# Two buffers for the rotated parts of q and k, and a block's rest behind the next block's tail, in a fused transformer layer

## The chip, the cores and the metric

The kernel runs on one core of one Trainium2 chip. The metric is the device time of one execution in microseconds (us). Three runs of the kernel before took 3130.38, 3134.19 and 3142.39 us; the median is 3134.19 us.

## What is computed

The input is 16 batches of 512 tokens with 512 channels, all in 32-bit floats. Each batch passes through an attention layer and a feed-forward layer, each with a layer norm before it and one behind it (a "sandwich"):

```
x = x + layernorm(attention(layernorm(x)))
x = x + layernorm(ffn(layernorm(x)))

attention: q, k, v = x @ W.T + b            # 32 heads of 16 channels
           q, k = rope(rope(q)), rope(rope(k))   # two rotations by position
           softmax(q k^T / 4, causal) v, then @ Wo.T + bo
ffn:       silu(x gate^T * gate_s) * (x up^T * up_s), 1408 wide
           then @ down^T * down_s           # weights are -1, 0 or 1
```

The two rotations are folded into one table of cosines and sines, so that a rotated value is y * cos + swap(y) * sin, where swap exchanges the halves of a block of 128 channels.

## The kernel before, in words

**Engines and order.** The program is written for one core with five engines: TensorE (PE) multiplies, ScalarE (ACT) and VectorE (DVE) work on PSUM and SBUF, GpSimd (POOL) on SBUF, SyncE (SP) issues nearly all DMAs. Every instruction goes through `InOrder` (line 43), so each engine executes in the order of the program. That order is made by hand. The attention of batch b is cut into 8 groups of 4 heads, and each group into 5 steps (`one_step`, line 841). A step issues the score products of one group (`scores`, line 569: `st` for the weights, `s` for the row maxima) and then the next piece of a list of dense work (`run_list`, line 741), which shares the list out over the steps by cost: a matmul of q, k, v or o costs 1, one of gate, up or down 0.27, a transpose 0.15. The list that runs beside batch b holds the o product and the whole feed-forward of batch b-1 and the v, q and k products of batch b+1 (`dense`, line 504; `gate_ups`, line 755; `downs`, line 772). Inside `dense` the order is: 4 blocks of v, 4 of q, 4 of o, then 4 of k, each k block behind the transposes of one block of 128 tokens for the feed-forward.

**Deferred work.** `merge(L, f, after)` puts a function into the list that `laid` (line 483) places once `after` units of cost have gone by behind the point where it was merged. That is how the follow-up work of a block lands some matmuls later in every engine's order.

**A block of q or k** (`qk_block`, line 331) is 4 matmuls into one PSUM buffer of the pool `ps_d`, which has 3 buffers and also serves v, o, gate, up, down, the transposes (`px`) and the turned maxima (`pm`). Three functions follow:

- `tail`, with the last matmul: ACT writes both swapped halves with the bias into `ys`; DVE computes `ya` = (p + bias) * cos, which frees the PSUM buffer; POOL computes `ys` *= sin and `ya` += `ys`.
- `rest`, merged at 3: ACT copies `ya` into `yh`, rounded to the form that fast matmuls take; POOL computes the remainder `yl` = `ya` - `yh`.
- `store`, merged at 5.5: SP issues four DMAs, two for `yh` and two for `yl`, to DRAM (`qd` or `kd`), from where `load_group` (line 556) fetches them for the scores of the next batch.

`ya` and `ys` have one buffer each, `yh` and `yl` two each. The sums of the down product use a tag "y" of their own with two buffers (`down`, line 434); their stores go to the output.

**The row maxima.** DVE reduces the scores `s` into `nm` (line 648), PE turns them (`pm`), DVE splits them into `nmhl`, and SP puts them into `mx` (line 669) for the weights of the following group.

**The front** (line 861) runs before the first step: it normalizes and transposes batches 0 and 1, computes q and k of batch 0 block by block, and checks between the blocks that all feed-forward weights are unchanged by rounding (`check_weights`, line 200: an ACT copy and a DVE comparison for each piece). The comparisons end in a flag that selects between two versions of the rest of the program; with these weights it is the one with rounded operands. Batch 0's own list (`first_list`, line 937) holds the q and k of batch 1. At the end the last batch's dense work runs alone (`last_list`, line 813).

In `dense` and in `first_list` the two deferred parts of a block are placed by the same two lines:

```
self.merge(L, rest, 3)
self.merge(L, store, 5.5)
```

Of the kernel before, what the change touches and what calls it, by code (L numbers as in the profile page):

```python
# [18 lines left out]
P = 128  # L19
T = 512  # L20
# [37 lines left out]
class Block:  # L58
# [199 lines left out]
    def turn(self, tiles, key, tb, to, big):  # L258

        st = {}  # L260

        def go(c):
            if c == 0:
                st["p"] = self.psum("px")
            self.pe.transpose(st["p"][:, ts(c, P)], tiles[key, tb][:, ts(c, P)], self.ident)
            if c == NC - 1:
                del tiles[key, tb]
                p = st["p"].rearrange("p (c t) -> p c t", c=NC)
                if big == "xntf" and self.exact:
                    if tb == 0:  # L270
                        to[key] = [self.tile([P, NC, T], big + i, bufs=1, dtype=FR) for i in ("", "l")]
                    hi, lo = (t[:, :, ts(tb, P)] for t in to[key])
                    self.act.copy(hi, p)
                    self.dve.tensor_tensor(lo, p, hi, ALU.subtract)
                    return
                if tb == 0:
                    to[key] = self.tile([P, self.NF if big == "ht" else NC, T], big, bufs=1)[:, 0:NC, :]
                self.act.copy(to[key][:, :, ts(tb, P)], p)

        return [(TR, lambda c=c: go(c)) for c in range(NC)]  # L280
# [50 lines left out]
    def qk_block(self, b, name, c):  # L331

        bias = self.col["b" + name]
        st = {}

        def tail(p):
            ya = st["a"] = self.tile([P, T], "ya", bufs=1)
            ys = st["s"] = self.tile([P, T], "ys", bufs=1)
            for h in range(2):
                i, o = slice(64 * h, 64 * h + 64), slice(64 - 64 * h, 128 - 64 * h)  # L340
                self.act.activation(ys[o, :], p[i, :], AF.Identity, bias=bias[i, c : c + 1])
            self.dve.scalar_tensor_tensor(ya, p, bias[:, c : c + 1], self.cos, ALU.add, ALU.mult)
            self.pool.tensor_tensor(ys, ys, self.sin, ALU.mult)
            self.pool.tensor_tensor(ya, ya, ys, ALU.add)

        def rest():
            ya = st["a"]
            hi, lo = st["y"] = [self.tile([P, T], n, bufs=2, dtype=FR) for n in ("yh", "yl")]
            self.act.copy(hi, ya)
            self.pool.tensor_tensor(lo, ya, hi, ALU.subtract)  # L350

        def store():
            i = (b % 2) * NC + c
            for part, y in enumerate(st["y"]):
                if name == "q":
                    d = self.qd[i][:, part, :].rearrange("(h r) t -> h r t", r=DH)
                else:
                    d = self.kd[i][part].rearrange("(h r) t -> h r t", r=DH)
                for h in range(2):
                    self.sp.dma_start(out=d[:, 8 * h : 8 * h + 8, :], in_=y[64 * h : 64 * h + 64, :].bitcast(FP))  # L360

        return self.product(
            "p" + name, NC, lambda i: self.wts[b, name, c // 2][:, i, ts(c % 2, P)], lambda i: self.xnts["a", b][:, i, :], tail
        ), rest, store
# [139 lines left out]
    def dense(self, b, between=()):  # L504


        L = []
        nxt, old = b + 1 < self.B, b >= 1
        o, bn = b - 1, b + 1
        do = lambda f, *args: L.append((0, lambda: f(*args)))  # L510

        def qk(name, c):
            items, rest, store = self.qk_block(bn, name, c)
            L.extend(items)
            self.merge(L, rest, 3)
            self.merge(L, store, 5.5)

        if nxt:
            for tb in range(NB):
                L += self.v_block(bn, tb)  # L520
            for c in range(NC):
                if c < 2:
                    do(self.load_w, o, "o", c)
                qk("q", c)
                if c % 2:
                    do(self.load_w, bn, "k", c // 2)
        else:
            for half in range(2):
                do(self.load_w, o, "o", half)
        later = []  # L530
        if old:
            do(self.load_xr, o, 0)
            do(self.load_xr, o, 1)
            for tb in range(NB):
                items, *rests = self.o_block(o, tb)
                L += items
                for r, k in zip(rests, (3.5, 6.5, 9.5)):
                    if r is rests[2] and tb >= 2 and nxt:
                        later.append(r)
                    else:  # L540
                        self.merge(L, r, k, ("f", tb))
        L += between
        for c in range(NC):
            if old:
                if c < 2:
                    do(self.load_wf, o, c)
                L.append(("need", ("f", c)))
                L += self.turn(self.xns, ("f", o), c, self.xnts, "xntf")
                if c < len(later):
                    self.merge(L, later[c], 5, ("f", c + 2))  # L550
            if nxt:
                qk("k", c)
        return L
# [307 lines left out]
    def front(self):  # L861

        nc = self.nc
        self.load_checks()
        checks = self.check_weights()

        def check(n):
            for _ in range(min(n, len(checks) - 1)):
                checks.pop(0)()

        def norm(b, tb):
            xt = self.xts.pop((b, tb))
            mr = self.stats(xt)

            def rest():
                xn = self.xns[("a", b), tb] = self.tile([P, C], "sg" if b and tb >= 2 else "xn", bufs=2)
                if b == 0:
                    self.dve.tensor_scalar(xn, xt, mr[0], mr[1], ALU.mult, ALU.add)
                else:
                    self.scaled(xn, xt, mr)  # L880

            return rest

        def turn(b, tb):
            for _, f in self.turn(self.xns, ("a", b), tb, self.xnts, ("xnta", "xntf")[b]):
                f()

        rest = None
        for tb in range(NB):
            now = norm(0, tb)  # L890
            if tb:
                rest()
                turn(0, tb - 1)
            rest = now
        rest()
        turn(0, NB - 1)
        for k in range(2):
            r = [norm(1, 2 * k), norm(1, 2 * k + 1)]
            check(1)
            for f in r:  # L900
                f()
        rests = []
        for name in "qk":
            for c in range(NC):
                items, rest, store = self.qk_block(0, name, c)
                for _, f in items[:2]:
                    f()
                for f in rests:
                    f()
                for _, f in items[2:]:  # L910
                    f()
                rests = [rest, store]
                if name == "q" and 1 <= c < 3:
                    for k in range(2):
                        turn(1, 2 * (c - 1) + k)
                check(2)
            if name == "q":
                for half in range(2):
                    self.load_w(0, "v", half)
            else:  # L920
                self.sp.dma_start(out=self.xn1, in_=self.xnts["a", 1])
        for f in rests:
            f()
        check(len(checks))
        nc.vector.tensor_scalar_mul(self.gh, self.col["gs"], 0.5)
        nc.vector.tensor_tensor(self.gu, self.gh, self.col["us"], ALU.mult)
        for tb in range(NB):
            for _, f in self.v_block(0, tb):
                f()
            if tb == 2:  # L930
                checks.pop(0)()
        self.wts[1, "v", 0], self.wts[1, "v", 1] = self.wts[0, "v", 0], self.wts[0, "v", 1]
        for tb in range(2):
            for _, f in self.v_block(1, tb):
                f()

    def first_list(self):

        L = []
# [11 lines left out]
        def qk(name, c):  # L951
            items, rest, store = self.qk_block(1, name, c)
            L.extend(items)
            self.merge(L, rest, 3)
            self.merge(L, store, 5.5)

        for c in range(NC):
            if c < 2:
# [4 lines left out]
        for c in range(NC):  # L963
            st = {}
# [127 lines left out]
```

## Time and profile before

| | us |
|---|---|
| median of three runs | 3134.19 |
| the profiled execution | 3133.78 |
| its span in the trace | 3132.0 |
| TensorE busy / idle in the span | 3028.9 / 103.1 |
| VectorE, ScalarE, GpSimd busy | 1901.4, 1540.6, 1559.8 |
| one batch in the middle (from v block to v block) | 186.7 to 188.4 |
| the front, up to the last weight check | 74.6 |

The profile is one execution recorded by the hardware. A row of the wait table says which engine, about to write which buffer, stood idle until which engine had written which buffer, with the total in us, the number of times and the longest. In a row of a stretch (from:to), each engine's busy time is followed by its number of instructions in brackets; then come the granted clock of TensorE (1.00 is full), the mean busy share of the DMA engines and the GB/s. In the chain, each line is a start, a duration and what was done. PEld is the loading of weights into TensorE, which overlaps its matmuls. Nearly all instructions carry line 53, since one helper issues them all, so that buffers are told apart by their names: `pq` and `pk` are the PSUM buffers of q and k blocks, `px` of transposes, `ht` and `xntfl` in the front hold weights to be checked.

### The profile page before, as it was taken

Reading aid. Unit: us, or ns where it says so; the run is one execution under the profiler, and the core shown is the slowest. Engines: PE = TensorE matmul, PEld = TensorE weight load, DVE = VectorE, ACT = ScalarE, POOL = GpSimd, SP = SyncE. Lnnn points to the kernel's source line nnn. Section 1 sums busy time; section 2 is a strip of 40 time slices with the busy share of each in tenths; the row PEclk is TensorE's granted clock in tenths of the full one; section 3 lists DMA queues with packets and bytes.
Section 4 is the critical chain, followed back from the end, with each engine's and each line's share of the span. In section 5 each row is a group of like instructions: output and inputs, shape, how many; then the busy total and the mean of one; then the engine's idle time right before and its main releaser. Section 6 shows DMA issues by size and latency. Waiting matters only on the chain.

```text
span 3132.0 us, 58833 instructions
## 1 busy us (share of the span) xinstructions
PE 3028.9 (97%) x20746; PEld 1726.6 (55%) x20746; DVE 1901.4 (61%) x6042; ACT 1540.6 (49%) x2243; POOL 1559.8 (50%) x2313
## 2 busy tenths in 40 slices
PE   6989999999999999999999999999999999999998
PEld 3334655646556464655646556464655646555556
DVE  6565656656566665656666565665656666566733
ACT  5354555554544545545554554545455454554432
POOL 6244456453654635456463654635456463653442
PEclk9889999999999999999999999999999999999999
DMA  7454535445353544535445353543535445343432
GB/s 262 173 195 134 197 102 170 149 144 177 129 184 99 172 157 130 199 103 172 144 144 179 130 189 102 164 154 130 200 102 171 144 144 183 124 158 113 133 102 72
DMA packets 228464, 471.90 MB, mean 151 GB/s; under 512 B 40976, under 2 KB 46096, under 8 KB 227728
## 3 DMA queue, kind: packets, MB, share of 16 engines
q1 hardware_dynamic: 227728, 466.99, 45.0%
q8 instruction: 167, 2.74, 0.4%
q10 hardware_dynamic: 432, 1.05, 0.1%
q14 instruction: 137, 1.12, 0.1%
HBM read 345.79 MB, written 125.30 MB: 150 GB/s over the span
## 4 chain that ended last, share of the span: by engine, by line
PE 76%; POOL 9%; DVE 8%; ACT 3%; DMA 2%; issue 2%; SPq 0%; POOLq 0%; DVEq 0%; ACTq 0%
PE st L53 13%; PE pg L53 11%; PE pu L53 11%; PE pd L53 9%; PE av L53 8%; PE pq L53 7%; PE pv L53 7%; PE po L53 4%; PE s L53 3%; PE pk L53 3%; DVE ln_st L53 2%; POOL ln_mv L53 2%; POOL x L53 2%; ACT pt L53 1%; DVE s L53 1%
## 5 line engine op out<-in xcount | busy, mean ns | idle before, releaser
L53 DVE CUSTOM_DVE_ANT_0 s<-s,mask 128x512 f32<-128x512 f32 (+1 forms) x1782 | 872.1, 519 | 622.5 <-PE s L53 564.2
L53 ACT ACTIVATE pt<-st 128x1024 f32<-128x1024 f32 (+1 forms) x640 | 601.4, 940 | 789.3 <-PE st L53 532.5
L53 POOL TENSOR_SCALAR_AFFINE_SELECT pt<-pt 128x256 f32<-128x256 f32 x1024 | 402.8, 409 | 1047.1 <-ACT pt L53 1041.4
L53 PE MATMUL s<-kh,q 32*128 32x512 f32 (+1 forms) x1782 | 344.5, 386 | 12.0 <-DVE nm L53 10.0
L53 PE MATMUL av<-pt,v 128*32 128x512 f32 (+3 forms) x4096 | 332.8, 443 | 0.0
L53 POOL TENSOR_TENSOR hl<-ht,hh 128x512 fp32r<-128x512 f32 (+1 forms) x192 | 232.2, 1210 | 191.1 <-ACT hh L53 171.0
L53 PEld LDWEIGHTS st<-mx,one 2*128 2x128 f32 x1280 | 119.3, 183 | 371.7 <-issue 201.3
L53 PE MATMUL st<-mx,one 2*128 2x512 f32 (+1 forms) x1280 | 307.2, 476 | 16.5 <-ACT pt L53 7.6
L53 PE MATMUL s<-kl,q 32*128 32x512 f32 (+1 forms) x1782 | 302.1, 327 | 1.0 <-DMA kl<-kd 1.0
L53 PE MATMUL st<-q,kl 32*128 32x512 f32 (+3 forms) x1792 | 297.1, 326 | 0.0
L53 PE MATMUL pd<-wd,hl 128*128 128x512 f32 x704 | 289.1, 411 | 7.0 <-POOL hl L53 6.8
L53 PE MATMUL pg<-xntf,wf 128*128 128x512 f32 x704 | 286.1, 406 | 2.2 <-ACT xntf L53 2.2
L53 PE MATMUL st<-q,kh 32*128 32x512 f32 (+3 forms) x1792 | 287.7, 330 | 0.0
L53 PE MATMUL pd<-wd,hh 128*128 128x512 f32 x704 | 285.0, 405 | 2.2 <-ACT hh L53 2.2
L53 DVE DVE_READ_ACCUMULATOR2_ANT nm<- 128x1 f32 x2048 | 285.2, 139 | 1.4
L53 PE MATMUL pg<-xntfl,wf 128*128 128x512 f32 x704 | 284.6, 404 | 0.5 <-DVE xntfl L53 0.5
L53 PE MATMUL pu<-xntfl,wf 128*128 128x512 f32 x704 | 279.8, 397 | 0.0
L53 PE MATMUL pu<-xntf,wf 128*128 128x512 f32 x704 | 279.7, 397 | 0.0
L53 PE MATMUL pk<-xnta,w 128*128 128x512 f32 x480 | 246.4, 643 | 12.0 <-DVE ya L53 12.0
L53 PE MATMUL pq<-xnta,w 128*128 128x512 f32 x480 | 238.6, 629 | 6.7 <-ACT xntf L53 6.0
L53 PE MATMUL po<-w,oc 128*128 128x512 f32 x512 | 240.8, 607 | 4.0 <-DMA w<-in_wo 4.0
L53 PE MATMUL pv<-w,xnta 128*128 128x512 f32 x464 | 220.9, 612 | 3.3 <-DVE ya L53 2.7
(126 smaller groups left out, 5520.6 us busy)
## 6 DMA issues: line engine op xcount, KB each, us to landing
wf<-wgs SPq DMA_DIRECT2D x176, 512.0 KB
q<-qd SPq DMA_DIRECT2D x128, 256.0 KB
kh<-kd SPq DMA_DIRECT2D x128, 256.0 KB
kl<-kd SPq DMA_DIRECT2D x128, 256.0 KB
od<-ot SPq DMA_DIRECT2D x128, 256.0 KB
w<-in_wo SPq DMA_DIRECT2D x34, 512.0 KB
xr<-in_x SPq DMA_DIRECT2D x66, 256.0 KB
w<-in_wq SPq DMA_DIRECT2D x32, 512.0 KB
```

What stands on the lines that cost most here:

```text
L53: return self.tc.keep_in_program_order(f(*args, **kwargs))
```

## The change

The buffer `ya` takes the tag "y" of the down sums, with its two buffers, in place of a buffer of its own; `ys` gets two buffers. The memory used stays the same. In both lists a block's `rest` is merged at 4.2 instead of 3, which is behind the tail of the next block (after its last matmul if transposes lie in between, otherwise after the first matmul of the block after it), and its `store` at 6.5 instead of 5.5. In the front, the rest and store of a block come behind all four matmuls and the tail of the next block, and the transposes of batch 1 come ahead of the q blocks 1 and 2 instead of behind them.

```diff
         def tail(p):
-            ya = st["a"] = self.tile([P, T], "ya", bufs=1)
-            ys = st["s"] = self.tile([P, T], "ys", bufs=1)
+
+            ya = st["a"] = self.tile([P, T], "y", bufs=2)
+            ys = st["s"] = self.tile([P, T], "ys", bufs=2)
...
             L.extend(items)
-            self.merge(L, rest, 3)
-            self.merge(L, store, 5.5)
+
+            self.merge(L, rest, 4.2)
+            self.merge(L, store, 6.5)
...
         for name in "qk":
             for c in range(NC):
+                if name == "q" and 1 <= c < 3:
+                    for k in range(2):
+                        turn(1, 2 * (c - 1) + k)
                 items, rest, store = self.qk_block(0, name, c)
-                for _, f in items[:2]:
+                for _, f in items:
                     f()
                 for f in rests:
                     f()
-                for _, f in items[2:]:
-                    f()
                 rests = [rest, store]
-                if name == "q" and 1 <= c < 3:
-                    for k in range(2):
-                        turn(1, 2 * (c - 1) + k)
                 check(2)
```

The pair of `merge` lines changes in the same way in `first_list`.

More of the change, by code (lines that the diff above doesn't have):

```diff
@@ L953, in qk @@
             L.extend(items)
-            self.merge(L, rest, 3)
-            self.merge(L, store, 5.5)
+            self.merge(L, rest, 4.2)
+            self.merge(L, store, 6.5)
         for c in range(NC):
```

## The prediction

> **What bounds the kernel now.** I read the page first, then TensorE's (PE's) waits, then the span cut into batches, then the chain and five-microsecond windows around the one place where PE stands still, and last the front.
>
> ```profile
> span 3132.0 us, 58833 instructions
> ...
> PE 3028.9 (97%) x20746; PEld 1726.6 (55%) x20746; DVE 1901.4 (61%) x6042; ACT 1540.6 (49%) x2243; POOL 1559.8 (50%) x2313
> ```
>
> PE is the bound, and 103 us of its span are idle. A change that adds no PE work can gain only that idle time and time at a low clock. The waits of PE:
>
> ```profile
> engine line waited for: us in total, times, longest us
> PE s L53 <- DVE nm L53: 13.8, 28, 1.2
> PE pk L53 <- DVE ya L53: 13.0, 13, 1.0
> ```
>
> The second row is the change's own subject: 13 waits of 1.0 us, one in each of batches 1 to 13. Two batches side by side:
>
> ```profile
> core 0: us, PE busy (x) PEld busy (x) DVE busy (x) ACT busy (x) POOL busy (x), PEclk, DMA share, GB/s
> 437.93:624.67 186.74, 184.78 (x1297) 106.44 (x1297) 116.25 (x375) 95.28 (x139) 96.86 (x144) 1.00 0.46 152
> 624.67:813.09 188.42, 186.53 (x1298) 106.92 (x1297) 116.31 (x375) 95.18 (x139) 96.81 (x144) 0.99 0.46 150
> ```
>
> Both idle for 1.9 us. The second is 1.7 us longer because PE is *busy* 1.75 us longer for the same matmuls: the clock. Where that is:
>
> ```profile
> 699.00:704.00 5.00, 4.48 (x29) 2.11 (x27) 3.18 (x11) 3.58 (x5) 4.91 (x6) 1.00 0.24 82
> 704.00:709.00 5.00, 4.00 (x7) 1.63 (x6) 3.54 (x12) 2.22 (x4) 4.56 (x6) 0.66 0.14 41
> ```
>
> PE idles 0.52 us, then 1.00 us, and then runs at a granted clock of 0.66 over 5 us (0.52 in the 2.5 us from 705.0). POOL is full (4.91 of 5.00). The chain through it:
>
> ```profile
> 700.75 1.28 POOL ya L53
> 702.03 0.72 POOL pt L53 x2
> 702.75 0.01 issue
> 702.77 1.28 POOL yl L53
> 704.05 0.14 issue
> 704.19 0.76 DVE ya L53
> 704.95 0.04 issue
> 705.00 4.54 PE pk L53 x6
> ```
>
> This is the k phase (k0 to k3 of the next batch). k2's product is ready at 701.5. ACT, next in line for it, sits in k1's copy `yh` for `ya` (idle 1.34 us), so k2's `ys` run only from 702.71 to 704.10. DVE's `ya` of k2 then starts at 704.19, also held by k1's `yl` until 704.05, since there is one `ya`. Only that frees the PSUM buffer that k3 needs. The 0.52 us before it has the same root: DVE stood 2.84 us (to 699.48) for k0's `yl` with the reductions of `s` queued behind.
>
> **The change part by part.**
>
> *Two buffers and the rest behind the next tail, batches 1 to 13.* I walk the k phase again with the durations of these rows. k1's `ys` end at 697.87 as now; its `ya` no longer waits for k0's `yl`, so DVE is done at 698.65 instead of 700.2, and the 0.52 us go. POOL's order is now `ys`1, `ya`1, then `yl`0: 698.2 + 3 x 1.27 = 702.05. `ya`2 waits for that `yl`0 (two buffers back), but also for k2's `ys`, which ACT can start at 701.6 and end at 703.0; cover 0.9 us. `ya`2 ends at 703.75. PE reaches k3 at 704.0 - 0.5 = 703.5, so some 0.25 us of wait stay. Per batch: 1.00 + 0.55 - 0.25 = 1.3; times 13 = **17 us**. From both sides: 0, if `yl`0 comes over 1 us later than walked, and 20.
>
> *The clock.* In 2.5 us windows, 8 of these 13 batches show a stretch down to about half clock (near 330, 706, 894, 1269, 1644, 2019, 2207, 2582 us), each right after this stall and nowhere else in the batch. One costs 1.75 us (the two rows above): 14 us. Here the Trainium skill speaks against the gain: "TensorE: Matmul & The Clock Gate", section on HAM oscillation, gives as the rule that only PE gaps above some 3.4 us cool the clock, so a gap of 1 us should not, and taking it away should not help: then the sum ends at 3117. The trace has the low clock behind gaps of 0.5 and 1.0 us, 8 times in 13. I take the trace: **14 us**; bounds 0 and 14.
>
> *Batch 14* has two 0.6 us waits `s <- DVE nm` in its k phase and one such stretch (2774): 0 to 2.9, I take **1.5 us**, as their cause is not shown as clearly.
>
> *ACT's new order.* `yh` (0.62 us) now follows the next tail's two `ys` (1.38) directly, 2.0 us in one piece before the next `pt`, which frees the only `st` buffer. The nearest row is `PE st <- ACT pt`, 7.6 us in 18 waits. Against it: ACT no longer idles for `ya` (153.6 us in 95 waits), and that idling stood in front of the same `pt`. Bounds: -3 and +8 (0.6 x 13); I take **2 us lost**.
>
> *SP.* The four store DMAs move a unit later (some 1.25 us), but `yl` comes 2.6 us later (702.05 for 699.45). SP, which now stands 2.1 us for k0's `yl`, will stand about 4, to 702.05, plus 1.2 for the two issues. Behind it lie the `mx` puts, issued at 705.16 when their data are ready, so they do not move; first use is at 715.29, and the landing on the chain at 237.44 took 4.04 us, so 5 us of cover are left. The next group's loads (712.23) and `wf` (709.11) lie later still. **0**; without the cover each us would be a us of PE per batch.
>
> *The shared tag "y".* q0's `ya` takes the buffer of a down sum whose store went out two steps into the list, while 16 units of v lie in between (20 us). **0**. The split pieces keep six units between a store and the reuse of its buffer, where they had five: **0**.
>
> *Batch 0's own list (80 to 250 us).* No PE wait there comes from `ya`, ACT never waits for POOL, and the end of the list runs everything left in its last step in both versions, so the 3.8 us wait for `mx` at 237 stays. **0**; but about 22 us are lost there to half clock, whose phases can shift: -5 to +5.
>
> *The front (16 to 75 us).* Read as a chain, a k block takes 5.07 us (POOL 57.05 to 62.12), of which ACT's `yh` and two hand-overs lie between POOL's steps. With the rest behind the next tail the period would be POOL's own 3 x 1.27 + 0.3 = 4.1: seven periods, 6.7 us. But look at DVE's weight checks beside POOL:
>
> ```profile
> 36.19 1.26 POOL L53 TENSOR_TENSOR yl<-ya,yh 128x512 fp32r<-128x512 f32 x1 [0.99 <-ACT yh L53]
> 36.22 0.08 DVE L53 DVE_READ_ACCUMULATOR xntfl<-xntfl,pt 128x1 f32 x1
> 36.22 2.32 DVE L53 SCALAR_TENSOR_TENSOR ht<-ht,pt 128x1024 f32<-128x1024 f32 x1
> ```
>
> The check starts 0.03 us after POOL and ends 1.09 us after it: it did nothing meanwhile. The Trainium skill, "SBUF — State Buffer", section "Who interferes with whom", has the rule: a DVE instruction with two SBUF inputs and a POOL instruction share a port as an exclusive lock, and whichever is second waits in full. So the two add up: 24 POOL steps x 1.27 = 30.5, 9 wide checks x 1.1 = 9.9, 11 narrow x 0.62 = 6.8, together 47.2 of the 47.6 us from the first POOL step (26.95) to the last check (74.50). The port is full already, and no order shortens it. The moved transposes wait on nothing new. By the chain 6.7 us, by the lock 0.4; I take **1 us**, bounds -2 and 7.
>
> **Sum.** 17 + 14 + 1.5 - 2 + 1 = 31.5. The profiled execution took 3133.8 (span 3132.0 and 1.8 around it), 0.4 under the median of three, 3134.2. 3133.8 - 31.5 = 3102.3, on the median's footing 3102.7, say 3103.
>
> **The rivals.**
>
> *The port is not the front's bound* (0.12): the front gains 7 instead of 1: 3097, with the best of the other terms 3088. For: 5.07 us is also exactly its chain. Against: the sum of 47.2.
>
> *A shorter stall keeps the low clock* (0.14). If 0.5 us of idling are enough to trip it, the 14 us stay and only the stall goes: 3103 + 14 = 3117; with half of the stall left (8.5), 3125. For: only 8 of 13 stalls trip it, so it is near an edge. Against: the 0.3 us wait later in each batch never does.
>
> *The wait only moves* (0.05): POOL is full for 14 us in each k phase, and the change takes no work off it. If `yl`0 falls behind the walk by over 1 us, `ya`2 waits for it as it now does for `yl`1: 3134. Against: two buffers give it a whole block more.
>
> *Slower* (0.05): SP. Walked, it is free again at 703.3 and the `mx` put goes at 705.16; to land (4.04) before 715.29 the put may go as late as 711 or so. If `yl`0 came 7 us later than walked, `mx` would begin to miss its group's first step; at 9 us PE would stall 2 us in place of 1.55, and each time long enough for a low clock: 13 x 0.45 + 5 x 1.75 = 15 us, so 3149. Against: the longest that anything stood for `yl` in this place is DVE's 2.84 us.
>
> *Forecast* (0.64): 3103, by itself 3093 to 3113.
>
> **How the numbers follow.** Times within 0.5% (15.7 us) count as no change, about what a measurement of this kernel can tell. Faster takes the forecast, the front case and over half of the low-clock case: 0.64 + 0.12 + 0.08 = 0.84. Same: 0.06 + 0.05 = 0.11. Slower 0.05. The range goes from the front case's best, 3088, to the half-left stall, 3125.
>
> **What would show it.** PE's waits: `pk <- DVE ya` gone or below 0.3 us each, `s <- DVE nm` down from 28 waits to about 14. Batches 2 to 12 at 185.0 to 185.5 us each, clock 1.00 throughout. `ACT yh <- POOL ya` (153.6) close to nothing, `DVE ya <- POOL yl` (68.3) below 20. The last weight check ends at 73 to 75 us. I am wrong if batches stay above 186.5 us; if a new PE wait of over 0.5 us per batch stands on `pt`, `mx` or `ya`; or if the front's end moves by over 3 us.

## The result, and the profile after

| | us |
|---|---|
| kernel before, four runs beside it | 3136.9 (3130.4 to 3142.4) |
| changed kernel, four runs | 3174.7 (3161.0 to 3193.5) |
| ratio | 1.0119, 95% interval 1.0090 to 1.0149 |
| profiled execution of the changed kernel, its span | 3174.1, 3172.2 |

The change costs 38 us where a gain of 31 was forecast, and the time lies outside the range. The page of the changed kernel:

```profile
span 3172.2 us, 58925 instructions
...
PE 3049.0 (96%) x20746; PEld 1733.6 (55%) x20746; DVE 1911.7 (60%) x6042; ACT 1535.9 (48%) x2243; POOL 1561.9 (49%) x2313
```

PE's matmuls are the same in number. They are busy 20 us longer, and PE is idle 123 us in place of 103. What PE waits for, whole span:

```profile
engine line waited for: us in total, times, longest us
PE s L53 <- DMA kl<-kd: 22.6, 30, 2.0
...
PE st L53 <- DMA mx<-nmhl: 9.5, 2, 6.8
...
PE s L53 <- DMA kh<-kd: 6.7, 7, 1.3
...
PE pk L53 <- DVE y L53: 2.4, 12, 0.2
```

The last row is the wait that the change was about (`ya` is named `y` now): 2.4 us for 13.0, at most 0.2 us each. In its place PE waits 29 us for `kl` and `kh`, the low and high parts of k that are fetched from DRAM for the scores. In the kernel before these waits were 2.7 us, none of them in batches 1 to 13. Batches 1 to 13 in one stretch, the kernel before:

```profile
243.19:2686.00 2442.81, 2417.86 (x16850) 1388.54 (x16848) 1511.58 (x4860) 1237.52 (x1806) 1256.62 (x1869) 0.99 0.46 151
```

and the changed kernel:

```profile
260.37:2727.10 2466.73, 2425.92 (x16851) 1391.03 (x16849) 1518.83 (x4860) 1233.39 (x1806) 1254.81 (x1869) 0.99 0.45 149
```

So 23.9 of the profiled execution's 40.2 us lie in these batches (15.9 of them idle, 8.0 busy), 17.2 ahead of them, and -0.9 behind. A mean batch takes 189.8 us for 187.9.

The place of the new wait in one batch, which starts at 646.12. The end of the chain of waits through it:

```profile
740.27 5.76 DMA kl<-kd
746.04 0.04 issue
746.08 0.33 PE s L53 x2
```

PE stood 1.77 us for that load of `kl`. It was issued late. SP's own queue in the changed kernel:

```profile
730.77 0.44 SPq L53 DMA_DIRECT2D wf<-wgs  x1
734.56 1.18 SPq L53 DMA_DIRECT2D kd<-yh  x2
737.92 1.18 SPq L53 DMA_DIRECT2D kd<-yl  x2
739.21 0.40 SPq L53 DMA_DIRECT2D q<-qd  x1
739.65 0.58 SPq L53 DMA_DIRECT2D kh<-kd  x1
740.27 0.60 SPq L53 DMA_DIRECT2D kl<-kd  x1
```

and in the kernel before, in the batch that starts at 624.67:

```profile
709.11 0.45 SPq L53 DMA_DIRECT2D wf<-wgs  x1
709.66 1.19 SPq L53 DMA_DIRECT2D kd<-yh  x2
710.95 1.19 SPq L53 DMA_DIRECT2D kd<-yl  x2
712.23 1.28 SPq L53 DMA_DIRECT2D q<-qd  x1
713.55 0.60 SPq L53 DMA_DIRECT2D kh<-kd  x1
714.20 0.60 SPq L53 DMA_DIRECT2D kl<-kd  x1
```

The order is the same: the store of block k2, then the three loads of a group of heads. What differs is that SP now stands for both halves of the store: until 734.56 for `yh`, though it was free at 731.21, and then 2.2 us for `yl`. Counted from the start of the batch, the store begins at 88.4 us in place of 85.0 and `kl` is asked for at 94.2 in place of 89.5: 3.4 us later for `yh`, 2.1 more for `yl`, 0.9 less for the shorter issue of the load of `q`, 4.6 in all. Its first use lay 4.2 us behind its landing before (724.14 - 714.20 - 5.76 to land, taking the duration after for both), so the cover is gone. The first use also comes 1.3 us earlier in the batch now (98.2 us after its start for 99.5: PE idles 0.4 us less up to there and is busy 0.9 less): 4.6 + 1.3 - 4.2 = 1.7, which is PE's wait. Why `yh` and `yl` are late, on ACT and POOL:

```profile
732.50 1.39 ACT L53 ACTIVATE ys<-pk,cols 64x512 f32<-64x512 f32 x2
733.91 0.62 ACT L53 CAST yh<-y 128x512 fp32r<-128x512 f32 x1
```

```profile
733.97 1.29 POOL L53 TENSOR_TENSOR ys<-ys,turn 128x512 f32<-128x512 f32 x1 [1.02 <-ACT ys L53]
735.35 1.29 POOL L53 TENSOR_TENSOR y<-y,ys 128x512 f32<-128x512 f32 x1
736.59 1.30 POOL L53 TENSOR_TENSOR yl<-y,yh 128x512 fp32r<-128x512 f32 x1
```

This `yh` and `yl` are k2's; the `ys` in front of the one and the two steps in front of the other are k3's. That is the change: k2's rest now stands behind k3's tail on ACT and POOL, and k3's tail waits for k3's four matmuls. POOL even idles 1.02 us for k3's `ys` while k2's `y` has long been complete. And behind that store, on an engine that issues in order, stand loads that have nothing to do with it.

Behind the wait the clock drops (2.5 us of the same batch):

```profile
747.50:750.00 2.50, 2.50 (x7) 1.96 (x6) 1.87 (x7) 1.20 (x2) 0.77 (x2) 0.50 0.70 277
```

### The profile page after: what moved, and what is told of

The parts are those of the page before. It is cut to its first block, busy times and chain, and to the rows that moved or that the text cites. A ratio compares the mean times of both kernels' runs of the same rounds, so it can differ in the third digit from the quotient of the medians.

```text
span 3172.2 us, 58925 instructions
## 1 busy us (share of the span) xinstructions
PE 3049.0 (96%) x20746; PEld 1733.6 (55%) x20746; DVE 1911.7 (60%) x6042; ACT 1535.9 (48%) x2243; POOL 1561.9 (49%) x2313
## 4 chain that ended last, share of the span: by engine, by line
PE 75%; DMA 9%; POOL 6%; ACT 3%; DVE 2%; issue 2%; SPq 2%; POOLq 0%; ACTq 0%; DVEq 0%
PE st L53 12%; PE pg L53 10%; PE pu L53 10%; PE pd L53 9%; PE av L53 8%; PE pq L53 7%; PE pv L53 7%; DMA kl<-kd 5%; PE pk L53 4%; PE po L53 3%; PE s L53 3%; SPq L53 2%; POOL y L53 1%; DMA wf<-wgs 1%; ACT pt L53 1%
## 5 line engine op out<-in xcount | busy, mean ns | idle before, releaser
L53 PE MATMUL pk<-xnta,w 128*128 128x512 f32 x480 | 235.1, 617 | 2.3 <-DVE y L53 2.2
L53 PE MATMUL pv<-w,xnta 128*128 128x512 f32 x464 | 230.1, 633 | 4.9 <-DMA w<-in_wv 3.4
```

The lines of the kernel that those rows point to most:

```text
L53: return self.tc.keep_in_program_order(f(*args, **kwargs))
```

## The experiments

**Theory and rivals.** The theory is SP's order: the stores of the third blocks, q2 and k2, wait for a later product and hold the group loads behind them; undo that, and the forecast gain appears. Where an expectation says A, it means this, together with a cold clock that the changed front leaves for the time ahead of batch 1 (the "prologue"). The rivals: the shared tag or the buffers themselves cost something (B); the changed front costs it, and the batches are only disturbed by it; the store's own later place costs it (D); or ACT's and POOL's new order does, whatever SP does (C).

All kernels from here have the two buffers. The first four split the change:

```diff
 e1_bufs_only: the buffers alone, positions as before
-            ya = st["a"] = self.tile([P, T], "ya", bufs=1)
-            ys = st["s"] = self.tile([P, T], "ys", bufs=1)
+            ya = st["a"] = self.tile([P, T], "y", bufs=2)
+            ys = st["s"] = self.tile([P, T], "ys", bufs=2)
 e2_lists_only: the front of before; in both lists
-            self.merge(L, rest, 3)
-            self.merge(L, store, 5.5)
+            self.merge(L, rest, 4.2)
+            self.merge(L, store, 6.5)
 e3_front_only: the changed front; in both lists 3 and 5.5
 e4_late_store: the changed kernel, but in both lists
-            self.merge(L, store, 6.5)
+            self.merge(L, store, 9)
```

> Two buffers for both rotated parts (tag y shared with the down sums), every position as before. Theory A (the changed kernel loses because stores whose yl now comes behind the next block's ys and ya hold the SP queue ahead of the group loads, and because its front starts the prologue with a cold clock): no loss here, 3125 to 3140 us, ratio 0.997 to 1.001; the ya wait of 1.0 us per batch stays, since ACT still sits in yh until ya is there, but the 0.55 us s wait shrinks. Rival B (sharing the tag makes down sums and q/k blocks wait for one another): part of the loss is here already, 3150 or more. Rival C (the new order on POOL and ACT itself delays pt): as before, 3130 to 3140.

> The changed kernel with the front of before: two buffers, rest at 4.2 and store at 6.5 in both lists. Theory A: the batches keep their new loss of about 2 us each (24 us in all, waits s <- kl and s <- kh at the two group loads behind the q2 and k2 stores), the front's part goes: 3155 to 3163. If the prologue's 12 us come from the first list's own stores and not from the front: 3168 to 3178. Rival B: 3160 to 3175, with waits of y for down stores.

> The changed front and two buffers, but rest at 3 and store at 5.5 in both lists. Theory A: front 1 to 2 us later (flag at 76 to 77 us for 75.1), the prologue up to 12 us longer where its matmuls fall into half clock, the batches as before at 186.7 to 188.4: 3140 to 3153. If the prologue's loss comes from the first list: 3135 to 3140.

> The changed kernel with the stores at 9 instead of 6.5, so that k2's store lies behind the group load and the others find yl ready: nothing else moves. Theory A: s <- kl and s <- kh drop from 29 us to under 8, batches 2 to 12 come down from 190 to 185.5 us or near it, 3110 to 3130 in all with the front's 16 us still lost. Rival C (POOL and ACT order itself): batches stay at 189 to 191, 3165 to 3180.

**e1: 3134.8, ratio 0.9995 (0.9986 to 1.0004).** The rival of the shared tag falls: buffers and tag cost nothing. They gain nothing either. Where the kernel before had two stalls, of 0.52 and 1.00 us, this one has one of 1.82:

```profile
703.76 2.84 PE L53 MATMUL pk<-xnta,w 128*128 128x512 f32 x6 [1.82 <-DVE y L53]
```

ACT shows why:

```profile
700.83 0.62 ACT L53 CAST yh<-y 128x512 fp32r<-128x512 f32 x1 [1.43 <-POOL y L53]
701.48 1.39 ACT L53 ACTIVATE ys<-pk,cols 64x512 f32<-64x512 f32 x2
```

It still stands in k1's `yh` in front of k2's `ys`. A second buffer is of no use while an engine that works in order waits between the two.

**e2: 3176.0, 1.0125 (1.0108 to 1.0142).** The loss is there without the changed front, so the lists make it, and the front falls as its cause. The 3155 to 3163 on record for A missed by 13 us; the time lies in the range of the case that puts the loss ahead of batch 1 on the first list, 3168 to 3178, which e10 tests.

**e3: 3141.1, 1.0015 (1.0006 to 1.0023).** The front alone costs about 5 us.

**e4: 3126.1, 0.9964 (0.9950 to 0.9978).** One number, the store's, turns a loss of 38 us into a gain of 10 to 11. A batch takes 186.0 us. But `store` moves the stores of all blocks, so the next two take the pair apart:

```diff
 e5_rest_only: front of before, in both lists
-            self.merge(L, rest, 3)
+            self.merge(L, rest, 4.2)
 e6_store_only: front of before, in both lists
-            self.merge(L, store, 5.5)
+            self.merge(L, store, 6.5)
```

> Front of before, two buffers, rest at 4.2, store at 5.5 as before, in both lists. If the loss comes from yl arriving later than the queue of SP reaches its store (theory A): SP stands at the stores at least as long as in the changed kernel, 3172 to 3195. If it comes from the later position of the store (rival D): 3130 to 3140.

> Front of before, two buffers, rest at 3 as before, store at 6.5, in both lists. Theory A: yl is ready when SP comes to the store, no loss: 3128 to 3142, with the pk wait of before. Rival D: 3155 to 3180.

**e5: 3163.9, 1.0089 (1.0072 to 1.0107).** The later rest alone makes most of the loss, with batches of 189.7 us, though the time is 8 us under the 3172 to 3195 on record. ACT's order and SP's are not parted by this run.

**e6: 3141.6, 1.0016 (1.0008 to 1.0025).** The later place of the store alone costs 5 us, and the stall of e1 stays (22.4 us in 13 waits). On top of the later rest it costs 12 (e2 against e5), where the later rest alone costs 27. So the store's own move is not the main cause: it is the later *product* that counts. Two runs ask how much the late store gives with the old front, in both lists and in one:

```diff
 e7_late_store_old_front: both lists
+            self.merge(L, rest, 4.2)
+            self.merge(L, store, 9)
 e8_late_store_dense_only: only the lists that run beside batches 1 to 13; the first and batch 14's as before
+            self.merge(L, rest, 4.2 if bn < self.B - 1 else 3)
+            self.merge(L, store, 9 if bn < self.B - 1 else 5.5)
```

> The late stores (rest 4.2, store 9, both lists) with the front of before. The front was measured as worth some 5 us by itself: 3118 to 3125. Batches at 185.7 us, the two 7 us waits of the first list (kh at 198, mx at 248) still there if they come from the list's late stores.

> As the one before it, but only the lists of batches 1 to 13 have rest at 4.2 and store at 9; the first list and batch 14's keep 3 and 5.5. If the first list's own stores make the losses ahead of batch 1: batch 1 begins at 241 to 245 us as before, batches at 185.7, the end as before: 3103 to 3112. If those losses come from elsewhere: 3116 to 3124.

**e7: 3122.9, 0.9951 (0.9935 to 0.9966). e8: 3107.9, 0.9911 (0.9895 to 0.9926).** e8 is the fastest kernel of this study, 28 us below the one before and 67 below the changed one, and near the 3103 that was forecast. The medians are 15 us apart, the profiled executions 13.9. Of these, 10.3 lie behind batch 13 (456.2 and 445.9 us from there to the end of the span): in e7 batch 14's list has 4.9 us of waits for `kh` there, in e8 0.4. Another 6.1 lie ahead of batch 1, and -2.5 between.

The last pair asks for the two stores alone, and for the first list alone:

```diff
 e9_two_stores_moved: e2, but in the lists beside batches 1 to 14
-            self.merge(L, store, 6.5)
+            self.merge(L, store, 9 if c == 2 else 6.5)
 e10_first_list_only: 3 and 5.5 in those lists; in the first list
-            self.merge(L, rest, 3)
-            self.merge(L, store, 5.5)
+            self.merge(L, rest, 4.2)
+            self.merge(L, store, 6.5)
```

> Two buffers, front of before, rest at 4.2, store at 6.5 in both lists, but in the lists of batches 1 to 14 the stores of block 2 of q and of k at 9: on SP this only exchanges each of these two with the group load behind it. If these two stores, standing in front of the loads, are the whole loss of the batches: batches 2 to 12 at 185.5 to 186.2 us instead of 190, total 3175 less 12 x 4, some 3122 to 3132. If the loss is spread over all the stores, the mx puts or DMA traffic: 3155 to 3175.

> Two buffers, front of before, rest at 4.2 and store at 6.5 in batch 0's own list alone; 3 and 5.5 in all other lists. If this list makes the changed kernel's losses ahead of batch 1: 3143 to 3152. If these come from the front or are chance of the clock's phases: 3132 to 3140.

**e9: 3119.4, 0.9944 (0.9931 to 0.9958).** This is the deciding run. ACT, DVE and POOL have the order of e2. On SP the stores of q2 and k2 change places with the group load behind them (in the k phase one load of `wf` goes along with the group), and nothing else moves. The time falls by 56.6 us against e2, 4 us for each of 14 lists, to 3 us under the 3122 to 3132 on record. ACT's and POOL's order falls as a cause. SP in e9 (the batch starts at 623.21):

```profile
711.95 0.37 SPq L53 DMA_DIRECT2D q<-qd  x1
712.36 0.58 SPq L53 DMA_DIRECT2D kh<-kd  x1
712.98 0.60 SPq L53 DMA_DIRECT2D kl<-kd  x1
...
718.02 1.29 SPq L53 DMA_DIRECT2D kd<-yh  x2
```

`kl` is asked for 89.8 us into the batch, where it was before the change. The waits of PE from 262 to 2660 us, in e9:

```profile
PE s L53 <- DVE nm L53: 5.7, 13, 0.5
PE st L53 <- ACT pt L53: 5.0, 14, 0.6
PE pk L53 <- DVE y L53: 1.5, 3, 0.7
PE s L53 <- DMA kl<-kd: 0.2, 1, 0.2
```

Of the old wait 1.5 us are left, of the new one 0.2. Batches 1 to 13 of e9:

```profile
250.51:2668.00 2417.49, 2404.50 (x16851) 1383.38 (x16850) 1520.97 (x4860) 1232.48 (x1806) 1250.36 (x1869) 1.00 0.46 152
```

**e10: 3139.1, 1.0007 (0.9998 to 1.0015).** No clear difference: the median is 2.5 us higher, within the noise and in the range for the case that this list does not make the loss ahead of batch 1. Still, a wait grows. In the first list k2's store now lies behind the last group's loads and so, together with k3's, in front of the last `mx` put. The put goes at 241.28 us in place of 236.78, and PE waits 7.2 us for it where it waited 3.8. Against PE, which is itself later here, the put is 1.0 us late; the other 2.4 us are its longer way, 7.3 us from issue to first use for 4.8.

## Why the prediction was wrong, point by point

**The stall at `ya`: right, but for the half microsecond in front of it.** `pk <- DVE` went from 13.0 us to 2.4, and at most 0.2 us a time, as walked (0.25). ACT's idle time for `ya` went from 153.6 to 6.8 us, DVE's for `yl` from 68.3 to 4.6. With SP out of the way (e9), batches 1 to 13 idle 13.0 us (2417.49 - 2404.50) for 24.9 before: 11.9 gained, for 15 forecast (17 less 2 for ACT's new order). In these batches `pk <- DVE` fell by 11.5 us, and `st <- ACT pt` is 5.0 us for 4.3 before, 0.7 for the 2 that were taken. But the wait of 0.52 us, which was to go with the stall, is for the most part still there: `s <- DVE nm` is 5.7 us in 13 waits for 7.1 in 13. It has another cause now, here in e9's batch that starts at 809.07:

```profile
888.34 1.27 POOL L53 TENSOR_TENSOR y<-y,ys 128x512 f32<-128x512 f32 x1
888.52 1.11 DVE L53 COPY nm<-nm 128x4 f32<-128x4 f32 x1
```

The copy of 4 columns starts 0.18 us behind POOL's sum and ends with it; at this place in the kernel before it took 0.16 us (700.75). It is the same in 11 of the 13 batches. So e9's batches 2 to 12 take 185.9 us each on average, above the 185.0 to 185.5 that were forecast.

**The clock: right.** The granted clock, added up in 2 us windows from 260 to 2660, cost 13.7 us before and 0.0 in e9; the forecast term was 14. The Trainium skill's rule ("TensorE: Matmul & The Clock Gate", section on HAM oscillation) that only gaps above some 3.4 us cool the clock would have made this 0. The trace was the better guide here: half clock follows in 7 of 13 batches of the changed kernel too, behind gaps of 1.2 to 1.9 us (one of them parted in two). In e8 and e9, where no gap in these batches is over 0.7 us, there is none. The rival "a shorter stall keeps the low clock" falls with it.

**SP, "0": the step that failed.** The prediction followed k0's store, found `mx` behind it with 5 us of cover, and dismissed the next group's loads with the words "lie later still". For k0 it was right: its `mx` put goes 80.5 us into the batch both before and after. But the loads lie behind *another* store: k2's, directly ahead of them, and in the q phase q2's. That store waits for `yh` and for `yl`, of which the prediction counted only `yl`, and the loads behind it had 4.2 us of cover where 4.6 were taken. There the price is not 0. Measured as changed kernel against e9 over batches 1 to 13:

| term | forecast us | measured us |
|---|---|---|
| stall and ACT's order (idle, before to e9) | -15 | -11.9 |
| clock (busy, before to e9) | -14 | -13.4 |
| SP: idle, e9 to after | 0 | +27.8 |
| SP: busy, e9 to after | 0 | +21.4 |
| sum | -29 | +23.9 |

The 27.8 us are (2466.73 - 2425.92) - (2417.49 - 2404.50): about two waits a batch, one for each phase, 25.8 us of them named `kl` and `kh`. Of the 21.4, 11.8 are the low clock that these waits bring back (the granted clock cost 13.2 us in the changed kernel's stretch and 1.4 in e9's, where it falls on the first microseconds of batch 1). The other 9.6 lie in the score products `s` and `st` of the steps that wait: 29 steps that idle longer than in e9 are also busy 10.9 us longer at full clock, 0.2 to 0.5 us each, and all others 1.2 us less. The wait parts products that overlap without it: `s<-kh` and `s<-kl` start 0.16 us apart at 723.98 before, 2.33 us apart at 743.75 after.

The rival "slower" named SP and the right mechanism, but put it on `mx` and on k0's store, and therefore asked for a `yl` 7 us later than walked. At k2, loads 4.6 us later were enough, as only 4.2 were in hand. The chance of 0.05 came from the wrong slack.

The signs of being wrong did show: batches stayed above 186.5 us (189.8), and a new wait of over 0.5 us a batch came, though on `kl` and not on one of the buffers that were named.

**The other rivals.** "The wait only moves" is not what happened to `ya`: that wait is gone. "The port is not the front's bound" falls: the front did not gain 7 us, the flag behind its last weight check moved from 75.1 to 76.7 us (77.3 in e3), inside the "3 us" that was named. POOL and DVE hold each other more than before: POOL's 24 steps of the front, 35.5 us in sum in the kernel before, are 40.2 us in the changed one. Its front:

```profile
45.98 2.28 DVE L53 SCALAR_TENSOR_TENSOR ht<-ht,pt 128x1024 f32<-128x1024 f32 x1
47.14 2.25 POOL L53 TENSOR_TENSOR ys<-ys,turn 128x512 f32<-128x512 f32 x1
```

Undisturbed, such steps take 1.2 to 1.3 us (in the kernel before DVE's at 19.46 took 1.22, POOL's at 26.95 1.28); where they overlap they take 2.3. So it was right to trust the shared port over the chain. Its term, though, was +1 us of gain, and e3 measured a loss of 5.

**Batch 0's list, "0": partly wrong.** "The end of the list runs everything left in its last step" holds, but k2's store is not at the end; it now stands in front of the last `mx` put (e10), and the wait of 3.8 us became 6.8 in the changed kernel. The bound of 5 us for the clock was too small as well: half clock cost TensorE 31.3 us between 80 us and batch 1, for 19.0 in the kernel before.

**Open.** 17 us of the profiled execution lie ahead of batch 1. Of these, 12.3 are the half clock of the last paragraph and 3.5 idle time. In the profile of after PE runs at half clock from 92 to 133 us, in that of before from 101 to 121. In the profiles of the ten experiments this loss to the clock lies between 10.8 us (e1) and 26.2 (e6), in no order that their edits explain. Runs of the front alone (+5) and the first list alone (+2.5, not clear of noise) do not add up to 17, and e2, with the old front, is as slow as the changed kernel. How much of the 17 is such a difference between executions and how much the change's was not settled. Nor is it known why half clock follows one gap and not the next of the same length.

## What to carry to other kernels

When a producer is moved later, look at every queue that waits for one of its products (here `yh` and `yl`) and list what stands *directly behind* that waiting instruction; for each of these, slack is first use minus landing, and it is this slack that the delay eats, even though the queue's order is unchanged. Do it for each repetition (all four blocks, both phases), because the one with the most behind it sets the price. A second buffer pays only when no engine that works in order still waits between the two uses, and a store that nobody needs soon is best placed behind the loads that somebody does.

## What the runs showed of the hardware

PE gaps of 1 to 2 us were followed by 3.4 us at half clock in about half of the batches (8 of 13 before, behind gaps of 1.0 us with 0.5 shortly ahead of them; 7 of 13 in e1 and in the changed kernel), and gaps of up to 0.7 us in none of 26 batches (e8, e9). That adds half as much again to the price of a short wait: in batches 1 to 13 of e2, 24.2 us of waits for `kl` and `kh` come with 11.9 us lost to the clock, and e9 has next to nothing of either.

A DVE copy of 4 columns took 1.11 us beside a POOL sum (e9), for 0.16 at the same place in the kernel before; POOL's sums and DVE's weight checks took up to 2.3 us where they overlapped, for 1.2 to 1.3 undisturbed.
